# Two graph layers with residual layernorms: layernorm from VectorE's statistics instruction and one scale-and-shift per batch

## The chip, the cores and the metric

The kernel runs on one core of a Trainium2 chip. A core has TensorE (PE in the profile; PEld is its weight load), VectorE (DVE), ScalarE (ACT), GpSimd (POOL), SyncE (SP) and 16 DMA engines. Each engine works through its own instructions in a fixed order and waits for others by semaphores. The metric is device time in microseconds (us), the median of several runs.

## The reference

```python
def _layernorm(x, axis=-1, eps=1e-5):
    m = jnp.mean(x, axis=axis, keepdims=True)
    v = jnp.var(x, axis=axis, keepdims=True)
    return (x - m) / jnp.sqrt(v + eps)
...
# x: (8, 2048, 128), adj: (2048, 2048), mostly zero
# layer 0
res = si[:, :, None] + sj[:, None, :] + relation[None] * w_r + g_b
agg = jnp.einsum('bij,bjd->bid', res, inputs)
return agg @ weight + bias
...
# layer 1, with A1 = A2 = adj, orders = 2
x1 = jnp.einsum('bnf,nw->bwf', x0, A)
x2 = 2.0 * jnp.einsum('bnf,nw->bwf', x1, A) - x0
...
out = jax.nn.relu(x @ Theta1 + bias)
...
x = _layernorm(x + layer0(x, adj))
x = _layernorm(x + layer1(x, adj, adj))
```

Both layers end in a residual sum and a layernorm over the last axis, 128 numbers for each of 2048 nodes and 8 batches.

## The kernel before

Nodes are cut into 16 chunks of 128. A tile of a chunk holds 128 nodes on the partitions and 8 batches x 128 features, 1024 fp32 numbers, along the free axis. `HB` is 4: most steps go by halves of four batches (`h` is 0 or 1)[...].

The work goes in four stages.

1. **Load, 0 to about 165 us.** Rows of adj and chunks of x are loaded; PE transposes adj's blocks and multiplies x by the weights into `Y`. Masks of the nonzero tiles are made.
2. **Chunks 0 to 3, dense, to about 285 us** (L758). Each of four chunks takes all 16 blocks of adj. Beside this, DVE and PE build lists of the rows that hold nonzeros.
3. **Layer 0 over twelve listed chunks, about 285 to 480 us.** `seq` gives their order. For each: `own_rows` multiplies by the diagonal block (L819), and `listed_rows` multiplies gathered rows by small blocks (L837): for each half four matmuls of 32 columns, two of 64 and one of 128, so fourteen in all. Seven gathers by POOL (L629) bring these rows, from a DRAM copy of Y, into nine buffers that go round; three more gathers a chunk bring the blocks for a later chunk. Each matmul shows as two records in the trace.
4. **Layer 1, two hops** over all chunks (`hop`), to about 725 and to the end. Their listed rows are gathered from `u_d`, the first product of layer 0's output, and from `y_d`, the first hop's output. The second hop ends in a sum with a bias (L895), a relu with the residual (L896), a layernorm and the store of the output.

What lies around the layernorm in stage 3: `finish0` adds PSUM and the residual in two halves (L371), then calls `layernorm`. Its result `z` goes to `make_u` only in the next turn, as `pending`: eight transposes (`pt_p`, in the helper at L182), copied by DVE and ACT in turn (L174 and L176), eight products with Theta (`pp`, L388), copies by ACT (L391) and a store to `u_d` (L392). Nothing of the first hop's gathers can start before all of `u_d` is written.

`layernorm` (L202 to L218) is a chain over two engines: sum over features (L205, DVE), mean (L208), subtraction (L209), then for each half a square on ACT (L213) and its sum on DVE (L214), a square root on ACT (L215), a reciprocal (L217) and a product (L218). The squares share one buffer, so the second square waits for the first sum.

```python
        for h in range(2):
            hs = slice(h * HB, (h + 1) * HB)
            sq = small.tile([P, HB, D], F32, name=f"sq_{name}_{h}", tag="sq", bufs=1)
            nc.scalar.activation(sq, z[:, hs, :], AF.Square)
            nc.vector.tensor_reduce(st[:, 2, hs], sq, AX.X, ALU.add)
```

It runs 32 times: for chunks 0 to 3 in stage 2, for the twelve listed chunks, and for all sixteen in the second hop. In stage 2 the argument `pin` puts the first instruction behind a given one in DVE's order.

What sets the order: a scheduler lays out each engine's instructions ahead of time, from its own costs. Some orders are fixed by hand: the matmuls of `own_rows` and `listed_rows` among themselves (`in_order`), all gathers on POOL among themselves (`gather`), SP's loads (`keep_in_program_order`). Where the transposes and products of `make_u` stand among these matmuls is left to the scheduler. In the kernel before, a turn of stage 3 has on PE: the eight 32-column matmuls of chunk c+1, some of the transposes of chunk c, the 64- and 128-column matmuls of chunk c+1, the other transposes, and the products `pp`, with `own_rows` of the chunk after that around them.

A branch at the end (`many`) holds a dense version for other data. It isn't taken here.

Of the kernel before, what the change touches and what calls it, by code (L numbers as in the profile page):

```python
# [8 lines left out]
F32 = mybir.dt.float32  # L9
I32 = mybir.dt.int32  # L10
AF = mybir.ActivationFunctionType
ALU = mybir.AluOpType
AX = mybir.AxisListType
# [5 lines left out]
def kernel(  # L19
# [29 lines left out]
    nc = tc.nc  # L49
    P = 128  # L50
    B, N, D = x.shape
    NC = N // P
    NG = NC // 4
    HB = B // 2
# [29 lines left out]
    small = ctx.enter_context(tc.tile_pool(name="small", bufs=2))  # L84
# [19 lines left out]
    def rows4(name):  # L104
        return w4.tile([P, B, D], F32, name=name, tag="w4")
# [29 lines left out]
    epst = const.tile([P, 1], F32)  # L135
# [58 lines left out]
    def behind(ins, prev):  # L194

        tc.add_manual_dep(
            ins.ins, prev.ins.name,
            mybir.DependencyInfo(mybir.DependencyClass.NoSync, mybir.DependencyReason.DATA),
            reason="order",
        )  # L200

    def layernorm(z, name, pin=None):  # L202

        st = small.tile([P, 4, B], F32, name=f"st_{name}", tag="st")
        head = nc.vector.tensor_reduce(st[:, 0], z, AX.X, ALU.add)  # L205
        if pin is not None:
            behind(head, pin)
        nc.vector.tensor_scalar(st[:, 1], st[:, 0], 1.0 / D, None, op0=ALU.mult)  # L208
        nc.vector.tensor_sub(z, z, st[:, 1][:, :, None].to_broadcast([P, B, D]))  # L209
        for h in range(2):  # L210
            hs = slice(h * HB, (h + 1) * HB)
            sq = small.tile([P, HB, D], F32, name=f"sq_{name}_{h}", tag="sq", bufs=1)
            nc.scalar.activation(sq, z[:, hs, :], AF.Square)  # L213
            nc.vector.tensor_reduce(st[:, 2, hs], sq, AX.X, ALU.add)  # L214
        nc.scalar.activation(st[:, 3], st[:, 2], AF.Sqrt, bias=epst, scale=1.0 / D)  # L215
        rs = small.tile([P, B], F32, name=f"rs_{name}", tag="rs")
        nc.vector.reciprocal(rs, st[:, 3])  # L217
        nc.vector.tensor_mul(z, z, rs[:, :, None].to_broadcast([P, B, D]))  # L218

    def load_x(c, name, q, t=None):  # L220
        if t is None:
# [145 lines left out]
    def finish0(c, accs, xr, norm=True):  # L367

        for h in range(2):
            hs = slice(h * HB, (h + 1) * HB)  # L370
            nc.vector.tensor_add(xr[:, hs, :], accs[h], xr[:, hs, :])  # L371
        if norm:
            layernorm(xr, f"0_{c}")
        return xr
# [19 lines left out]
    def copy_r(n0, n1):  # L394
# [22 lines left out]
        op0=ALU.mult,  # L417
# [288 lines left out]
    for c in range(ND):  # L706
# [15 lines left out]
        else:  # L722
            z = finish0(c, accs, xr, c > 2)
        if c + 1 < ND:
            accs1, sit = acc_pair(), si_t(c + 1)
            at2 = first_at.get(c + 2)
            for j in range(NC):
                if c == 0:
                    if j == 4:
                        tile_ranks()  # L730
                    if j == 7:
                        tile_lists()
                    if j == 10:
                        at = tile_lists_end()
                        half_ranks()
                    if j == 14:
                        chunk_ranks()
                        z = finish0(c, accs, xr, False)
                        layernorm(z, "0_0", at)
# [5 lines left out]
                if c == 2:  # L745
                    if j == 4:
                        at = chunk_lists_end()
                        layernorm(z1, "0_1", at)
                    if j == 8:
                        layernorm(z, "0_2", at)  # L750
# [93 lines left out]
    with nc.allow_non_contiguous_dma(reason="512-byte rows of a diagonal block"):  # L844
        fetch_own(0, y0_d, seq[0])
        xr = load_x(seq[0], "xs", nc.sync)
        for c, c1 in zip(seq, seq[1:] + [None]):
# [10 lines left out]
            z = finish0(c, accs, xr)  # L858
# [83 lines left out]
    with tc.If(many == 1), nc.allow_non_contiguous_dma(reason="512-byte rows of a block"):  # L942
        for c in range(NC):
# [3 lines left out]
            z = finish0(c, accs, xr)  # L947
            nc.scalar.dma_start(out=x1_d[c * P:(c + 1) * P, :], in_=flat(z))
            make_u(c, z, rows4(f"xtd{c}"))
        for i, src in ((1, u_d), (2, y_d)):  # L950
            for c in range(NC):
# [9 lines left out]
                z = rows4(f"zd{i}_{c}")  # L961
                for h in range(2):
                    hs = slice(h * HB, (h + 1) * HB)
# [45 lines left out]
```

## Time and profile before

| what | value |
|---|---|
| median of 5 runs | 910.82 us (905.13 to 915.06) |
| the profiled execution | 913.96 us |
| its span in the trace | 912.2 us |
| PE busy | 779.5 us, 85% of the span |
| DVE busy | 405.3 us, 44% |
| ACT busy | 175.3 us, 19% |
| POOL busy | 439.1 us, 48% |
| data moved by DMA | 265.05 MB, mean 291 GB/s |
| mean granted TensorE clock | 0.943 |

A row of the groups, the waits or the timeline names the line, the engine, the operation, and what it writes and reads (`out<-in`), with partitions x elements. In the timeline a row starts with its start and length in us, and may end in brackets with how long the engine had been idle before and who let it go on. The layernorm's own rows, from the groups (busy us, then mean ns of one, then idle before it):

```profile
L214 DVE TENSOR_REDUCE st<-sq 128x4 f32<-128x512 f32 x64 | 43.9, 685 | 57.2 <-ACT sq L213 39.0
L213 ACT ACTIVATE sq<-z 128x512 f32<-128x512 f32 x32 | 20.1, 630 | 161.7 <-DVE z L209 112.5
```

The granted clock is the share of full speed that the throttle left to TensorE. Idle time of an engine that isn't the bottleneck costs nothing.

### The profile page before, as it was taken

The page shows a single profiled execution, that of the slowest core. Times are in us where ns is not written, and L with a number is a line of the kernel's source. Part 1 is how long each engine was busy: PE and PEld are TensorE (multiplying, and loading weights), DVE is VectorE, ACT ScalarE, POOL GpSimd, SP SyncE. Part 2 cuts the span into 40 slices and gives each one's busy share as a digit, 9 for nine tenths or more (in the row PEclk, how much of TensorE's full clock was granted, in tenths as well). Part 3 has the DMA queues.
Part 4 walks back from the last instruction along what each step waited for, and adds up shares of the span by engine and source line. Part 5 has one row for each costly group of instructions (what it writes and reads, how often), then busy time and mean ns, then how long its engine had stood idle before and what let it go on. Part 6 is the DMA issues. An engine that isn't in the chain of part 4 may idle for free. (4 is left out here: it accounts for less than half of the span.)

```text
span 912.2 us, 10299 instructions
## 1 busy us (share of the span) xinstructions
PE 779.5 (85%) x3607; PEld 382.6 (42%) x3607; DVE 405.3 (44%) x639; ACT 175.3 (19%) x397; POOL 439.1 (48%) x431
## 2 busy tenths in 40 slices
PE   5999989999996868687887888887999889999992
PEld 4666664465443333332344232332343334455430
DVE  5456673448962634455652000000100065776775
ACT  3666651011111212121211000000000010111111
POOL 0000000036577766477622766676664565676750
PEclk9999998999997978887999899999999999999996
DMA  8699999872658987899976788888998889999992
GB/s 285 213 307 317 332 297 302 264 267 78 216 200 310 342 305 264 296 317 312 342 315 198 263 282 303 293 314 298 352 383 313 296 295 326 363 346 357 349 333 78
DMA packets 171416, 265.05 MB, mean 291 GB/s; under 512 B 17069, under 2 KB 122069, under 8 KB 169180
## 3 DMA queue, kind: packets, MB, share of 16 engines
q0 software_dynamic: 49280, 148.61, 45.6%
q1 hardware_dynamic: 98746, 87.98, 30.0%
q10 hardware_dynamic: 23330, 27.73, 8.5%
q8 instruction: 30, 0.49, 0.2%
q14 instruction: 30, 0.25, 0.1%
HBM read 241.63 MB, written 60.96 MB: 332 GB/s over the span
## 5 line engine op out<-in xcount | busy, mean ns | idle before, releaser
L837 PE MATMUL acc<-Y,rc 128*32 128x512 f32 (+2 forms) x896 | 244.7, 626 | 43.0 <-issue 18.4
L629 POOL DMA_INDIRECT Y<-y_d,idx x196 | 210.8, 1075 | 120.7 <-PE acc L837 58.1
L629 POOL DMA_INDIRECT stage<-rr_d,idx x84 | 88.0, 1047 | 229.4 <-PE acc L758 206.5
L629 POOL DMA_INDIRECT Y<-u_d,idx x112 | 110.9, 990 | 88.3 <-DMA u_d<-rc 31.3
L837 PEld LDWEIGHTS acc<-Y,rc 128*32 128x32 f32 (+2 forms) x896 | 62.5, 130 | 214.4 <-issue 133.4
L837 PE MATMUL acc<-Y,rct 128*32 128x512 f32 (+2 forms) x336 | 89.6, 686 | 7.6 <-DMA Y<-y_d,idx 5.6
L758 PE MATMUL acc<-Y,wide 128*128 128x512 f32 x192 | 87.6, 606 | 0.0
L214 DVE TENSOR_REDUCE st<-sq 128x4 f32<-128x512 f32 x64 | 43.9, 685 | 57.2 <-ACT sq L213 39.0
L819 PE MATMUL acc<-Y,rd 128*128 128x512 f32 x140 | 67.9, 597 | 0.0
L174 DVE COPY z<-acc 128x512 f32<-128x512 f32 x9 | 6.2, 692 | 136.9 <-remote 65.7
L758 PEld LDWEIGHTS acc<-Y,wide 128*128 128x128 f32 x192 | 36.0, 195 | 39.8 <-issue 39.8
L213 ACT ACTIVATE sq<-z 128x512 f32<-128x512 f32 x32 | 20.1, 630 | 161.7 <-DVE z L209 112.5
L837 PEld LDWEIGHTS acc<-Y,rct 128*32 128x32 f32 (+2 forms) x336 | 22.8, 144 | 60.5 <-issue 45.0
L182 PE MATMUL pt_a<-ident,rc 128*128 128x128 f32 x240 | 35.9, 286 | 6.6 <-DMA rc<-in_adj_dram 6.2
L319 PE MATMUL acc<-wx,tr_x 128*128 128x130 f32 x256 | 36.8, 287 | 4.2 <-ACT tr_x L176 3.4
L290 DVE TENSOR_REDUCE rc<-rc 128x64 f32<-128x2048 f32 x16 | 36.5, 2279 | 6.3 <-DMA rc<-in_adj_dram 6.3
L182 PE MATMUL pt_p<-ident,xs 128*128 128x128 f32 x96 | 16.0, 289 | 27.1 <-DVE xs L218 24.2
L319 PEld LDWEIGHTS acc<-wx,tr_x 128*128 128x128 f32 x256 | 32.9, 195 | 14.5 <-ACT tr_x L176 6.7
L329 PE MATMUL acc<-Y,wide 128*128 128x512 f32 x64 | 36.1, 646 | 2.5 <-ACT Y L323 1.4
L371 DVE TENSOR_TENSOR xs<-acc,xs 128x512 f32<-128x512 f32 x24 | 16.6, 692 | 48.1 <-PE acc L837 26.0
L298 DVE TENSOR_REDUCE stage<-rct 128x64 f32<-128x2048 f32 x12 | 27.4, 2286 | 20.5 <-ACT rct L176 20.5
L182 PEld LDWEIGHTS pt_a<-ident,rc 128*128 128x128 f32 x240 | 29.5, 148 | 16.0 <-issue 14.7
(204 smaller groups left out, 908.0 us busy)
## 6 DMA issues: line engine op xcount, KB each, us to landing
rc<-in_adj_dram SPq DMA_DIRECT2D x16, 1024.0 KB
rr_d<-rct SPq DMA_DIRECT2D x12, 1024.0 KB
rr_d<-in_adj_dram SPq DMA_DIRECT2D x12, 1024.0 KB
xs<-in_x_dram SPq DMA_DIRECT2D x20, 512.0 KB
y_d<-Y SPq DMA_DIRECT2D x16, 512.0 KB
out_dram<-z ACTq DMA_DIRECT2D x16, 512.0 KB
u_d<-u ACTq DMA_DIRECT2D x14, 512.0 KB
Y<-y_d SPq DMA_DIRECT2D x14, 512.0 KB
```

The lines of the kernel that those rows point to most:

```text
L182: nc.tensor.transpose(pt[:, i, :], s, ident)
L213: nc.scalar.activation(sq, z[:, hs, :], AF.Square)
L214: nc.vector.tensor_reduce(st[:, 2, hs], sq, AX.X, ALU.add)
L290: nc.vector.tensor_reduce(mk[:, c, :], a.rearrange("p (w f) -> p w f", f=TW), AX.X, ALU.max, apply_absolute_value=True,)
L298: nc.vector.tensor_reduce(mkt[:, :, 4 * c:4 * c + 4], at.rearrange("p j (t f) -> p j t f", f=TW), AX.X, ALU.max, apply_absolute_value=True,)
L319: nc.tensor.matmul(py[:, i, 0:D + 2], xt[b // HB][:, (b + i) % HB, :], wx, start=True, stop=True,)
L329: nc.tensor.matmul(acc0[h], first_at[0][:, c, :], Y[c][:, h * HB:(h + 1) * HB, :], start=(c == 0), stop=False, skip_group_check=True,)
L371: nc.vector.tensor_add(xr[:, hs, :], accs[h], xr[:, hs, :])
L629: g = nc.gpsimd.indirect_dma_start(out=out, out_offset=None, in_=src, in_offset=bass.IndirectOffsetOnAxis(ap=ids[:, n:n + 1], axis=0), bou ...
L758: mm = nc.tensor.matmul(accs1[h], at1[:, j, :], Y[j][:, h * HB:(h + 1) * HB, :], start=(j == 0), stop=False, skip_group_check=True,)
L819: in_order(nc.tensor.matmul(accs[h], r, t[:, h * HB:(h + 1) * HB, :], start=start, stop=False, skip_group_check=True,))
L837: in_order(nc.tensor.matmul(accs[h][w * t:w * t + w], r[:, o + w * t:o + w * t + w], gs[t][:, h * HB * D:(h + 1) * HB * D], start=False, s ...
```

## The change

Only `layernorm` is edited. The sums and squares go; VectorE's statistics instruction (`bn_stats`) is called once per batch on 128 numbers and writes six: a count, a mean and a sum of squared deviations for the numbers in even places, and the same for those in odd places. A few instructions on 8 numbers per partition join the two halves: the sum of squared deviations of all 128 is the sum of the two plus 32 times the squared gap between the means. From this come r = 1 / sqrt(variance + eps) and -m r. One instruction per batch then gives z r - m r in place, for batches 1, 4 and 6 on ACT and for the other five on DVE. The buffer of squares is no longer needed.

```diff
-        st = small.tile([P, 4, B], F32, name=f"st_{name}", tag="st")
-        head = nc.vector.tensor_reduce(st[:, 0], z, AX.X, ALU.add)
-        if pin is not None:
-            behind(head, pin)
-        nc.vector.tensor_scalar(st[:, 1], st[:, 0], 1.0 / D, None, op0=ALU.mult)
-        nc.vector.tensor_sub(z, z, st[:, 1][:, :, None].to_broadcast([P, B, D]))
-        for h in range(2):
-            hs = slice(h * HB, (h + 1) * HB)
-            sq = small.tile([P, HB, D], F32, name=f"sq_{name}_{h}", tag="sq", bufs=1)
-            nc.scalar.activation(sq, z[:, hs, :], AF.Square)
-            nc.vector.tensor_reduce(st[:, 2, hs], sq, AX.X, ALU.add)
-        nc.scalar.activation(st[:, 3], st[:, 2], AF.Sqrt, bias=epst, scale=1.0 / D)
-        rs = small.tile([P, B], F32, name=f"rs_{name}", tag="rs")
-        nc.vector.reciprocal(rs, st[:, 3])
-        nc.vector.tensor_mul(z, z, rs[:, :, None].to_broadcast([P, B, D]))
+        nb = z.shape[1]
+        st = small.tile([P, B, 6], F32, name=f"st_{name}", tag="st")[:, 0:nb]
+        for b in range(nb):
+            head = nc.vector.bn_stats(st[:, b], z[:, b])
+            if pin is not None:
+                behind(head, pin)
+        m0, m1, v0, v1, gap, var = [st[:, :, n] for n in (1, 4, 2, 5, 0, 3)]
+        nc.vector.tensor_sub(gap, m0, m1)
+        nc.vector.tensor_add(var, v0, v1)
+        nc.vector.scalar_tensor_tensor(gap, gap, D / 4.0, gap, op0=ALU.mult, op1=ALU.mult)
+        nc.vector.tensor_add(var, var, gap)
+        nc.scalar.activation(v0, var, AF.Sqrt, bias=epst, scale=1.0 / D)
+        nc.vector.tensor_add(m0, m0, m1)
+        nc.vector.reciprocal(v1, v0)
+        nc.vector.scalar_tensor_tensor(m1, m0, -0.5, v1, op0=ALU.mult, op1=ALU.mult)
+        for b in range(nb):
+            if b % 8 in (1, 4, 6):
+                nc.scalar.activation(
+                    z[:, b], z[:, b], AF.Identity, bias=m1[:, b:b + 1], scale=v1[:, b:b + 1]
+                )
+            else:
+                nc.vector.tensor_scalar(
+                    z[:, b], z[:, b], v1[:, b:b + 1], m1[:, b:b + 1], op0=ALU.mult, op1=ALU.add
+                )
```

No other line changes. The scheduler, whose costs see other instructions, lays out the engines anew: in a turn of stage 3, PE now has two of the 32-column matmuls of chunk c+1, the eight transposes of chunk c with one 32-column matmul among them, the other five, the products `pp` among the 64-column matmuls, and the 128-column ones last. POOL's and SP's orders are the same as before.

## The prediction

> **What bounds the kernel now.** I read the page's slices first, to see which stages have slack, then the stage table, PE's waits in the stage that has it, the timeline of one turn there, and the end of the timeline.
>
> ```profile
> PE   5999989999996868687887888887999889999992
> ...
> PEclk9999998999997978887999899999999999999996
> DMA  8699999872658987899976788888998889999992
> ```
>
> Each digit is 1/40 of the span. PE is full until slice 13 and again from slice 32 on. The hole in between has two parts: 285 to 480 us (layer 0 over the listed chunks, with a layernorm in each turn) and the first Chebyshev hop up to 725 us, which has no layernorm. So the change can act in the first part, and in the last digit, the end.
>
> ```profile
> 290.00:480.00 190.00, 145.84 (x680) 66.85 (x679) 94.95 (x160) 37.23 (x69) 115.13 (x106) 0.88 0.87 312
> 335.00:350.00 15.00, 10.15 (x45) 5.43 (x46) 7.00 (x12) 3.12 (x6) 5.98 (x5) 0.69 0.59 207
> 455.00:470.00 15.00, 10.48 (x60) 4.85 (x56) 9.61 (x17) 3.75 (x8) 5.97 (x5) 1.00 1.03 404
> ```
>
> These are rows of the stage table (window, length, busy PE, PEld, DVE, ACT, POOL, granted clock, DMA share, GB/s). PE is idle for 44 of 190 us, but the transfers are busy 0.87 of the time: twelve 15 us windows from 290 to 470 average 0.90, from 0.59 to 1.03. There is slack, and not much.
>
> ```profile
> PE pt_p L182 <- DVE xs L218: 24.2, 9, 4.5
> PE pp L388 <- DVE wide L174: 5.4, 1, 5.4
> PE pp L388 <- ACT wide L176: 4.1, 2, 2.1
> PE pp L388 <- issue: 4.0, 1, 4.0
> ```
>
> PE's waits from 290 to 500 us: 24.2 us for the layernorm's last instruction (L218), and 13.5 us before the products pp, whose input copies stand in DVE's and ACT's queues behind the sums of L371 or the squares. One turn shows the loop:
>
> ```profile
> 444.68 0.41 PE L182 MATMUL pt_p<-ident,xs 128*128 128x128 f32 x2 [2.99 <-DVE xs L218]
> 445.02 3.85 PE L837 MATMUL acc<-Y,rct 128*64 128x512 f32 x12
> 448.05 0.69 DVE L371 TENSOR_TENSOR xs<-acc,xs 128x512 f32<-128x512 f32 x1 [2.63 <-PE acc L837]
> 450.11 1.21 DVE L205 TENSOR_REDUCE st<-xs 128x8 f32<-128x1024 f32 x1
> 456.55 1.22 DVE L218 TENSOR_TENSOR xs<-xs,rs 128x1024 f32<-128x1024 f32 x1
> 457.93 0.41 PE L182 MATMUL pt_p<-ident,xs 128*128 128x128 f32 x2 [2.85 <-DVE xs L218]
> ```
>
> PE's order is fixed: the rest of the next chunk's matmuls stands behind the transposes of the last chunk's normalized rows. So a turn is sum, layernorm, transposes, 3.85 us of matmuls, sum: 13.25 us here. L205's first start is 300.0 and its twelfth 477.7, so the mean turn is 177.7/11 = 16.2 us.
>
> ```profile
> 493.77 0.98 POOL L629 DMA_INDIRECT Y<-u_d,idx  x1 [31.25 <-DMA u_d<-rc]
> ```
>
> The next hop's first gather waits until the last layernorm's product is stored: the end of that stage is a pure chain through it. So is the end of the kernel:
>
> ```profile
> 893.28 1.04 PE L894 MATMUL pt_r<-ident,Y 128*128 128x128 f32 x8
> ...
> 899.39 1.22 DVE L205 TENSOR_REDUCE st<-z 128x8 f32<-128x1024 f32 x1
> ...
> 902.17 0.63 ACT L213 ACTIVATE sq<-z 128x512 f32<-128x512 f32 x1 [6.70 <-DVE z L209]
> ...
> 904.21 0.69 DVE L214 TENSOR_REDUCE st<-sq 128x4 f32<-128x512 f32 x1 [0.70 <-ACT sq L213]
> ...
> 905.50 1.22 DVE L218 TENSOR_TENSOR z<-z,rs 128x1024 f32<-128x1024 f32 x1
> 906.76 0.38 ACTq L903 DMA_DIRECT2D out_dram<-z  x1
> ```
>
> PE ends at 894.3, but DVE still has a layernorm in hand and starts the last at 899.39. It takes 7.33 us to 906.72.
>
> **What the Trainium skill says.** "VectorE: DVE Perf Modes", The TRN2 errata: an fp32 tensor_tensor takes (N+151)/0.96 ns. The trace agrees: 692 for 512 columns, 1226 for 1024. The same page, The DRAIN you can't avoid: the next operation waits for the pipe, unless it is not held. Here independent 128x128 operations of 0.28 us start 0.20 apart (444.45, 444.65), dependent ones 0.02 to 0.03 after the other's end. "ScalarE: Activation LUTs", What ACT_TABLE_LOAD costs: 186 ns + 0.833 N, 93 more for each pointer operand, and back-to-back ones overlap by 93. The trace's L215 (N 8, one pointer) took 301, near the 286 of that. The same page, Table sets: identity is in every set, so no reload is due; the trace has one load before L215, of 1.283 us, and none later between square and square root. No page prices the statistics instruction.
>
> **The change, part by part.** Each of the 32 layernorms loses L205, L208, L209, two squares with their reductions, L217 and L218 (7.33 us as a chain, DVE 5.4 and ACT 1.56 us busy). It gains:
> - Eight statistics of 128 columns. No row shows one. At one column a cycle like L205 I take 0.20 apart and 0.29 each; below that 0.13 apart if it ran at two columns, above 0.33 if it goes over its data twice, 0.5 if worse. The first falls between the two sums; seven remain: 7 x 0.20 + 0.09 = 1.5 us.
> - Small 128x8 steps at L208's 0.17, two pairs overlapping: 0.6 us. Square root 0.30 and two handovers: 0.36. Reciprocal 0.20 and the product 0.17, with gaps: 0.42.
> - Apply: DVE 4 x 0.20 + 0.28 = 1.1 us; ACT three with two pointers, an estimate by the ScalarE page of 479 ns spaced 386: 1.25, with handover 1.3. They run side by side.
>
> Sum 4.2 us for 7.33, and busy DVE 4.9, ACT 1.74. ACT's extra 0.2 us lies in its idle time. I take no double rate for the pointer-scalar steps: L663, the same form, took 280 to 343 ns, no less than a tensor_tensor's 287.
>
> **End.** The last sums need PE's 894.3, so L896 ends at 895.0. DVE is free by then: the previous layernorm ends near 892 (884.9 + 2.6 of sums + 4.2). 895.0 + 8 x 0.20 + 0.09 + 2.7 = 899.4 for 906.7: **-7.3 us**. The last store behind it is unchanged.
>
> **Stage end.** From the last L371's end, 477.2, 4.2 us lead to 481.4; the transposes started at 485.94, behind PE work that ends near 480 in the new order. The stored product and the gather follow: **-4 us**.
>
> **Turns of the listed stage.** The scheduler also moves PE work: the transposes now stand behind only two of the eight 32-column matmuls, and six of these (1.92 x 6/8 = 1.4 us) and all of pp (1.8 us) come behind the transposes, ahead of the wider matmuls. POOL's and SP's orders are unchanged. So part of the gain is handed back. Old turn at full clock 13.25. New: transposes 0.9 + 1.4 + 1.8 + 3.4 of wider matmuls up to the first sum, then 0.9 to the second, 0.7 for it and 4.2: 13.3 by plain addition; transposes, products and matmuls overlap at their joints as these records do, so I take 12.6, 0.65 less, or 7 us over 11 turns. Still about 2.8 us of PE waiting per turn: the layernorm is shorter, but has less in front of it. What should go besides is part of the 13.5 us before pp, since pp's copies now have 1.4 us of matmuls as cover, and the squares no longer stand in ACT's queue. If that cover is gone, up to 13.5 us come back. The ceiling is the transfers: 180 us at 0.90 need 166 at 0.97, so at most 14 us. POOL is near too: ten gathers a turn, 1.05 + 0.30 each, make 13.5 us. Both are late next. I take **-8 us**, bounds -14 and +4.
>
> **Second hop.** From 725 to 880 us PE is busy for 151.2 of 155 and the transfers 0.96, DVE 102: the shorter layernorm is hidden. If that cover went, DVE's 6.8 us a chunk would still be under PE's 10. Zero; likewise before 285 us, where PE is busy for 117 of 125 (at best -2).
>
> Sum: -19.3 us against the profiled execution, 913.96 us (span 912.2): 894.7. That run was 0.3% above the median, 910.82, so the forecast is 910.82 x 894.7/913.96 = **891.5 us**.
>
> **Rivals**, in median time.
> - The stage gains nothing, since the transfers and POOL hold its turn: only the two chains, -11.3: 899.5. For it: windows at 0.97 to 1.03. Against: one at 0.59.
> - The stage reaches the transfers' ceiling and a cheaper statistic helps both chains: -14, -5, -8.5: 883.4.
> - A statistic goes over its data twice, 0.33 apart: turns lengthen by 0.9, past the 0.65 won, +3 us; the end gains 6.3, the stage end 3: about 904.5, no change.
> - **Slower**: the statistic costs 0.5 or more. The place is pt_p at L182. Each layernorm grows by 2.1 us, and PE, with the 3.2 us that used to precede or run beside it now behind the transposes, holds back the next chunk's sums and the gather buffers. It decides from 0.29 apart (0.65/7 above 0.20). At 0.5: turn +1.45 x 12 = +17; end -4.9, stage end -2: about +10, 921. If PE is at half clock in those 3.2 us too, +3 a turn, a dearer 0.33 would do.
> - That the change doesn't do what it says: no, both the instructions and their moved order are in the program.
>
> **How the numbers follow.** Changes within 1% can't be told from none (five runs spread from 905.1 to 915.1). Chances: forecast 0.57, no stage gain 0.18, ceiling 0.09, two passes 0.10, slower 0.06. Faster takes the first, the ceiling and half of the second: 0.76; slower 0.06; within 1% 0.18. The range, 877 to 905, takes in the ceiling with 6 us more of front and stage, and the two-pass case.
>
> **What would show it.** Statistics of 0.29 us starting 0.20 apart; last layernorm 4.2 us, from 895; PE's waits at pt_p still near 2.8 us a turn, those before pp gone; turns of about 15.5 us; the first gather of u_d some 12 us earlier; the second hop as long as before. Wrong if the statistic is over 0.3 apart, or if pt_p waits over 4 us a turn with POOL idle behind it.

## The result, and the profile after

The changed kernel takes **903.02 us** (median of 41 runs, 896.0 to 909.3). The kernel before takes 908.63 in the runs beside them (78 runs, 899.8 to 925.0). The medians differ by 5.6 us. The ratio is 0.9951, 95% interval 0.9935 to 0.9966, which is 4.5 us; it leaves out executions over 1.5% above the fastest of their kernel. Forecast were 19.3 us less, 891.5.

The profiled execution of the changed kernel took 901.61 us, 1.4 below its median; that of the kernel before took 913.96, 5.3 above its own. So the two traces differ by 12.3 us, more than the medians. First the slices of the changed kernel's page, to set beside those of before:

```profile
PE   5999989999992898989897878888988899999994
...
PEclk9999998999996899999999898989999999999998
DMA  8699999982567999999985788888999689999994
```

PE is fuller in slices 15, 17, 19 and 21, and one digit fell to 2: slice 13, at 270 to 292 us. The granted clock is higher in slices 15 to 20, where the kernel before has digits of 7 and 8. The stage table's row from 290 to 480 us (length, busy PE, PEld, DVE, ACT, POOL, clock, DMA share, GB/s) and PE's waits from 290 to 500 us:

```profile
290.00:480.00 190.00, 171.07 (x717) 72.90 (x718) 83.80 (x333) 41.63 (x87) 103.88 (x105) 0.98 0.91 319
```

```profile
PE pp L397 <- issue: 16.4, 1, 16.4
PE pt_p L182 <- issue: 10.6, 7, 2.5
PE acc L846 <- DMA Y<-u_d,idx: 6.1, 2, 3.4
PE pt_p L182 <- PE acc L846: 5.4, 4, 1.4
```

PE's 24.2 us before the transposes pt_p shrank to 16.0, and the small waits at pp are gone. But PE is busy for 171 us where it was for 146, which is 17% more, with 5% more matmul records in the window (717 for 680): the first sign that its matmuls cost more. And one wait of 16.4 us at pp is new. It ends at 292.8 and explains the digit 2 of slice 13.

The layernorm itself is as short as forecast. A row of the groups (busy, mean ns), then the end of the timeline and the first gather of the first hop:

```profile
L207 DVE BATCH_NORM_STATS2 st<-z 128x6 f32<-128x128 f32 x128 | 26.2, 278 | 0.0
```

```profile
486.51 0.99 POOL L638 DMA_INDIRECT Y<-u_d,idx  x1 [27.17 <-DMA u_d<-rc]
...
889.88 1.64 DVE L207 BATCH_NORM_STATS2 st<-z 128x6 f32<-128x128 f32 x8
...
892.98 1.37 DVE L225 TENSOR_SCALAR z<-z,st 128x128 f32<-128x128 f32 x5
...
894.43 0.38 ACTq L912 DMA_DIRECT2D out_dram<-z  x1
```

Eight statistics take 1.64 us, so they start 0.20 apart; the last layernorm goes from 889.88 to 894.35, 4.5 us (forecast 4.2).

The same kernels ran later on other chips. These come in two kinds: on the **slower** ones the kernel before takes 908 to 913 us, as in the result above, on the **quicker** ones 878 to 880. Cut at the same points, the traces give (us; the quicker chip's are the runs b_again and a_again below):

| stretch | slower: before, after | change | quicker: before, after | change |
|---|---|---|---|---|
| start to the first second-half sum of stage 3 | 299.3, 305.7 | +6.4 | 301.3, 300.6 | -0.7 |
| eleven turns | 177.2, 168.9 | -8.3 | 156.7, 164.7 | +7.9 |
| last sum to first gather of u_d | 17.2, 11.9 | -5.4 | 17.3, 11.9 | -5.4 |
| first hop | 217.3, 218.8 | +1.5 | 204.9, 204.9 | 0 |
| second hop to the last transposes | 182.2, 182.6 | +0.4 | 179.2, 182.7 | +3.5 |
| last transposes to last store | 13.5, 6.5 | -6.9 | 10.4, 6.5 | -3.8 |

The places where the gain goes are the turns, the front (the first row) and, on the quicker chip, the second hop.

### The profile page after: what moved, and what is told of

Read it like the earlier page. It is cut to its first block, busy times and chain, and to the rows that moved or that the text cites. A ratio compares the mean times of both kernels' runs of the same rounds, so it can differ in the third digit from the quotient of the medians.

```text
span 899.8 us, 10724 instructions
## 1 busy us (share of the span) xinstructions
PE 795.0 (88%) x3607; PEld 382.4 (42%) x3607; DVE 360.9 (40%) x1055; ACT 176.9 (20%) x429; POOL 420.4 (47%) x431
## 5 line engine op out<-in xcount | busy, mean ns | idle before, releaser
L638 POOL DMA_INDIRECT Y<-y_d,idx x196 | 194.7, 994 | 135.9 <-PE acc L846 74.5
L638 POOL DMA_INDIRECT stage<-rr_d,idx x84 | 84.9, 1011 | 229.5 <-DMA y_d<-Y 187.5
L846 PE MATMUL acc<-Y,rct 128*32 128x512 f32 (+2 forms) x336 | 105.5, 622 | 0.0
L828 PE MATMUL acc<-Y,rd 128*128 128x512 f32 x140 | 66.0, 593 | 0.0
L215 ACT ACTIVATE st<-st,epst 128x8 f32<-128x8 f32 x32 | 9.9, 309 | 234.6 <-DVE st L214 71.8
L380 DVE TENSOR_TENSOR xs<-acc,xs 128x512 f32<-128x512 f32 x24 | 16.4, 683 | 82.0 <-issue 36.0
L905 DVE SCALAR_TENSOR_TENSOR z<-z,pt_r 128x512 f32<-128x512 f32 x32 | 20.6, 683 | 51.7 <-PE pt_r L903 18.7
L328 PEld LDWEIGHTS acc<-wx,tr_x 128*128 128x128 f32 x256 | 32.9, 195 | 14.4 <-ACT tr_x L176 6.4
L885 PEld LDWEIGHTS acc<-th,wide 128*128 128x128 f32 x256 | 31.5, 192 | 8.1 <-issue 8.1
```

The lines of the kernel that those rows point to most:

```text
L328: nc.tensor.matmul(py[:, i, 0:D + 2], xt[b // HB][:, (b + i) % HB, :], wx, start=True, stop=True,)
L638: g = nc.gpsimd.indirect_dma_start(out=out, out_offset=None, in_=src, in_offset=bass.IndirectOffsetOnAxis(ap=ids[:, n:n + 1], axis=0), bou ...
L828: in_order(nc.tensor.matmul(accs[h], r, t[:, h * HB:(h + 1) * HB, :], start=start, stop=False, skip_group_check=True,))
L846: in_order(nc.tensor.matmul(accs[h][w * t:w * t + w], r[:, o + w * t:o + w * t + w], gs[t][:, h * HB * D:(h + 1) * HB * D], start=False, s ...
L885: in_order(nc.tensor.matmul(accs[h][:, b, :], x1t[c][:, h * HB + b, :], th[:, i, :], start=(b == 0), stop=False, skip_group_check=True,))
L905: nc.vector.scalar_tensor_tensor(z[:, hs, :], z[:, hs, :], 0.0, pt, op0=ALU.max, op1=ALU.add)
```

## What a turn of the changed kernel shows

One turn, 414.27 to 429.47 us, from the timelines of DVE and PE, and ahead of it a row of the kernel before. `x10` counts records, two to a matmul:

```profile
439.77 1.92 PE L837 MATMUL acc<-Y,rct 128*32 128x512 f32 x16
```

```profile
414.27 0.69 DVE L380 TENSOR_TENSOR xs<-acc,xs 128x512 f32<-128x512 f32 x1 [6.97 <-issue]
...
416.73 1.05 PE L846 MATMUL acc<-Y,rct 128*32 128x512 f32 x4
419.14 0.90 PE L182 MATMUL pt_p<-ident,xs 128*128 128x128 f32 x5 [1.35 <-PE acc L846]
419.98 1.04 PE L846 MATMUL acc<-Y,rct 128*32 128x512 f32 x2
420.95 0.55 PE L182 MATMUL pt_p<-ident,xs 128*128 128x128 f32 x3
421.43 1.90 PE L846 MATMUL acc<-Y,rct 128*32 128x512 f32 x10
423.26 0.94 PE L397 MATMUL pp<-th,wide 128*128 128x128 f32 x6
424.13 1.07 PE L846 MATMUL acc<-Y,rct 128*64 128x512 f32 x2
425.13 0.94 PE L397 MATMUL pp<-th,wide 128*128 128x128 f32 x6
426.00 1.93 PE L846 MATMUL acc<-Y,rct 128*64 128x512 f32 x6
427.86 0.71 PE L397 MATMUL pp<-th,wide 128*128 128x128 f32 x4
428.40 1.88 PE L846 MATMUL acc<-Y,rct 128*128 128x512 f32 x4
...
429.47 0.69 DVE L380 TENSOR_TENSOR xs<-acc,xs 128x512 f32<-128x512 f32 x1 [6.98 <-PE pp L397]
```

A single 32-column matmul (x2) takes 1.04 us, and five (x10) take 1.90. In the kernel before, all eight together (x16) took 1.92. They are meant to run four at a time, in four strips of columns: a **group** takes as long as one of its members. Here the transposes cut the eight into pieces of 2, 1 and 5: 1.05 + 1.04 + 1.90 = 4.0 us. The products cut the 64-column pairs likewise: 1.07 + 1.93 = 3.0 us for four, which need 1.9. The Trainium skill, "TensorE: Matmul & The Clock Gate", Packing small matmuls, says that matmuls in different strips overlap, and that PE never reorders matmuls. These rows agree with both.

So a turn is 4.87 us from the first sum to the transposes and 10.33 of PE without a gap from there to the next sum: 15.20. The eight turns from 338 to 460 us are 15.19 to 15.20 each, and so are eight in the changed kernel's trace on a quicker chip. The turns of the kernel before do not repeat like that: in its trace the eleven are 13.2 to 20.1 us long.

The granted clock is a second thing in which the old turns differ. The eleven turns of the kernel before and of the changed one (columns as in the stage table), and a row of wider matmuls of the kernel before, twelve records like those that took 3.85 us in the turn of the prediction:

```profile
299.30:476.50 177.20, 133.04 (x605) 59.04 (x604) 90.16 (x153) 34.89 (x65) 109.18 (x100) 0.87 0.88 315
```

```profile
305.70:474.60 168.90, 152.85 (x630) 62.82 (x630) 74.11 (x298) 37.23 (x78) 96.35 (x97) 0.99 0.91 323
```

```profile
397.43 6.17 PE L837 MATMUL acc<-Y,rct 128*64 128x512 f32 x12
```

From 395.4 to 402.2 us the granted clock was 0.50. In the trace of the kernel before, the three turns in which it never fell took 13.2, 13.4 and 14.0 us, the other eight 14.4 to 20.1. An estimate from the rows' means: a clock of 0.87 over 177 us costs up to 23 us of full-speed time, one of 0.99 over 169 us up to 2. On another slower chip the old turns had 0.91 (175.5 us, the run b2_again below). What makes the clock fall is not shown here.

## Experiments

Ratios are to the kernel before on the same chip, run beside each trial, with 95% intervals; a gain in us is taken from the ratio, unless two medians are named. First the parts alone, on a quicker chip. A line in `layernorm` sends some of its invocations to the old text, placed at the end of the file (its `st` has six rows in place of four, the rest is unchanged):

```diff
     def layernorm(z, name, pin=None):
+        if name[0] != "1": return layernorm_old(nc, small, behind, epst, z, name, pin)
```

That is the end alone; the others differ in the condition on the name.

**New in the second hop alone.**

> The new layernorm for the sixteen chunks of the second hop alone, the old one for all others. PE's order is then that of the kernel before. The prediction's end term says -7.3 us against the kernel before, all of it between the last PE work and the last store (in the traces that stretch fell from 13.5 to 6.6 us). Rival, the second hop is not free of the layernorm after all: then the change in time differs from -7 by over 2 us, and the stretch from the first gather of y_d to the last transposes (182.2 us before) moves.

Measured 0.9976 (0.9955 to 0.9996): -2.1 us, not -7.3. Two things account for the rest. On this chip the old end is short too: 10.8 and 11.0 us in the next two runs, 6.5 here. And the rival holds: the hop to the last transposes takes 181.4 us, against 177.9 and 179.6 in these two, which have the old layernorm there.

**New in the listed chunks alone.**

> The new layernorm for the twelve listed chunks of layer 0 alone. PE's order in the turns is then that of the changed kernel, the front's that of the kernel before. The prediction's two terms: turns -8, stage end -4, so -12 us. First rival, the time of the changed kernel is lost in the front: here -12 too, with the first sums (L380) near 298.6 us as in the kernel before, not 304.8. Second rival, the two traces are single executions and the turns gain little in the median: 0 to -3 us, with turns still at 15.4 us in some executions and over 16 in others.

Measured 1.0027 (1.0012 to 1.0042): slower by 2.4 us. Neither theory had that. The turns take 164.7 us, at 15.20 each, against 157.6 in the run before this one, whose turns are the old ones.

**New in the four dense chunks alone.**

> The new layernorm for the four dense chunks alone; beyond the first turn PE's order is that of the kernel before. Prediction: 0 (at best -2). First rival, the order of the front: the square root of chunk 3 now stands between the two copies of u1 on ACT, and the copy of chunk 2's transposes behind that layernorm on DVE, so +6 us, with PE standing some 16 us before pp and the first sums near 304.8 us instead of 298.6. Second rival, the late front of the changed kernel's trace is a matter of that one execution: 0, first sums near 298.6.

Measured 0.9942 (0.9922 to 0.9962): 5.1 us less; first sums at 298.4. On this chip the front isn't late. What the 5.1 us are isn't settled: this trace and the others of its kind differ by 2 us in the front and less elsewhere.

**New everywhere but there.**

> The new layernorm everywhere but for the four dense chunks. If the front's order costs 6 us, this is 6 us shorter than the changed kernel (903.0): near 897, -12 us against the kernel before; by the prediction's whole sum even -19, near 890. If the front costs nothing in the median, the same as the changed kernel, -5.6 us.

Measured 0.9998 (0.9984 to 1.0013). This is e1 and e2 added: -2.1 + 2.4.

**Both kernels again, on a quicker chip.**

> The kernel before, for a trace beside the others of this call; timed against itself it must give a ratio of 1. It gives the anchors (first sums, eleven turns, first gather of u_d, hops, end) on the chip on which the edits are run. If the end in it, from the last transposes to the last store, is 11 us instead of 13.5, the end term of the prediction was read from one execution.

> The changed kernel again, beside the others. If the turns are locked by PE's order, they are 15.20 us here as in the first trace, whatever the chip; if transfers set them, they are 14.3 or less, as those of the kernel with the new layernorm in the second hop alone. From the parts run alone (end -2.1, listed chunks +2.4, first four -5.1) the sum is -4.8 us against the kernel before; if parts don't add up, 0 or -10.

The kernel before against itself: 0.9994 (0.9975 to 1.0012). The changed kernel: 0.9995 (0.9978 to 1.0012), so **no gain at all** on this chip. The parts' sum, about -5 us, is not found again: they ran on one quicker chip and this on another, and which of the two, the chip or the sum, is at fault stays open. The end is indeed 10.4 us here and not 13.5; the turns are 15.19. From 300 to 455 us (columns as above), the kernel before and the changed one:

```profile
300.00:455.00 155.00, 131.62 (x608) 57.01 (x608) 90.09 (x153) 35.23 (x66) 109.85 (x100) 0.97 0.97 357
```

```profile
300.00:455.00 155.00, 141.82 (x586) 58.06 (x584) 70.54 (x288) 34.90 (x74) 96.56 (x97) 1.00 0.96 342
```

PE is busier by 10 us while fewer of its records (586 against 608) fall into the window.

**Whole groups.** PE's order in the listed turns, written by hand, with the new layernorm:

```diff
-            nc.tensor.transpose(pt[:, i, :], s, ident)
+            hold[0](nc.tensor.transpose(pt[:, i, :], s, ident))
...
     def make_u(c, z, xt, u=None, part=0):
+        hold[0] = in_order if part else (lambda mm: mm)
...
             gs = [rows_of(a + n * c + t) for t in range(n)]
+            n == 2 and mid and mid()
...
-            listed_rows(0, y0_d, c, accs)
-            make_u(*pending)
+            listed_rows(0, y0_d, c, accs, len(pending) == 4 and (lambda: make_u(*pending, 1)))
+            make_u(*pending, *[2][:len(pending) == 4])
```

Part 1 of `make_u` is the transposes, part 2 the products and the store. The lines on `hold` and the parts that are left out do the same for the products. The first listed turn keeps the scheduler's order.

> The changed kernel with PE's order in the turns written by hand: the eight 32-column matmuls together, then the eight transposes, the four 64- and two 128-column matmuls together, then the products. In the changed kernel's trace six 32-column matmuls behind the first transpose took 2.94 us, where all eight take 1.92 together, and a 64-column pair split by a product took 1.07 more. Theory, the split groups cost the turns about 3 us of PE on the path: turns of 13.0 to 13.5 us (ten gathers of 1.30 on POOL are then the bound), PE busy about 10.7 us a turn instead of 13.9, -20 us against the changed kernel. Rival, the transfers bind as soon as PE does not: turns of 14.3, -10 us. Second rival, the split does not matter and the layernorm's chain sets 15.2: no change.

Measured **0.9867** (0.9845 to 0.9889), -11.3 us between the medians, 866.8 and 878.1. The eleven turns take 153.1 us, 13.9 each: less than the rival's 14.3, and more than the 12.3 us a turn for which PE is busy. The transfers leave little room: over the eleven turns the DMA share is 0.99, against 0.96 over the old turns on this chip.

**The same order with the old layernorm.**

> The old layernorm everywhere, with the same order by hand for PE. If the order is worth the gain and not the layernorm, this is as fast as the new layernorm with that order, but for the end. By the chain, sums 1.6, layernorm 7.3, transposes 1.4 and 2.9 of wider matmuls make turns of 13.2 us: within 2 us of the kernel before, which had 13 to 14.3 on a chip like this. If the old layernorm's length counts in the turns, they are over 14.

Measured 0.9997 (0.9977 to 1.0018); turns 159.5 us, 14.5 each. So on this chip the order alone gives nothing and the layernorm alone gives nothing (0.9995), while both together give 1.3%: the short layernorm is worth something here only if PE's groups stay whole.

**Whole groups, but transposes and products early.** To tell the split from the new place of the transposes, this order keeps them ahead of the wider matmuls: four 32-column matmuls, the eight transposes, the other four, the products, then the rest.

```diff
             for h in range(2):
+                (n, h) == (4, 1) and mid and mid(1)
+                (n, h) == (2, 0) and mid and mid(2)
```

> The changed kernel with PE's order by hand, but close to its own: the transposes stand between the two halves of the 32-column matmuls and the products ahead of the 64-column ones, as in the changed kernel, only that no group of 32- or 64-column matmuls is split. If the split groups cost the time, the turn is 15.2 less some 3 us of PE on the path, so what the transfers allow: near 13.9 as in the other unsplit order, -10 us against the changed kernel. If the place of the transposes and products ahead of the wider matmuls costs it, turns stay near 15 and the time within 3 us of the changed kernel (0.9995 of the kernel before).

Measured **0.9803** (0.9762 to 0.9844), on a slower chip: 891.95 us for 910.16, where the changed kernel had 0.9951. Part of a turn:

```profile
402.88 1.31 PE L182 MATMUL pt_p<-ident,xs 128*128 128x128 f32 x8 [0.68 <-issue]
404.11 1.07 PE L847 MATMUL acc<-Y,rct 128*32 128x512 f32 x8
405.25 2.05 PE L397 MATMUL pp<-th,wide 128*128 128x128 f32 x16
407.23 3.85 PE L847 MATMUL acc<-Y,rct 128*64 128x512 f32 x12
```

Four 32-column matmuls (x8) take 1.07, as long as one took alone. The eleven turns take 161.2 us against 168.9, with transposes and products near the places that the changed kernel gives them, and with DVE's and ACT's order in a turn as in the changed kernel. Nor is it the granted clock, which is 0.97 from 300 to 470 us here and was 0.99 over the turns of the changed kernel. It is the split that costs, not the place.

The same kernel ran twice more on another slower chip, as a base for the next trials:

> The kernel with whole groups and PE's order close to the changed kernel's, once more, as the base of the next two: 0.980 to 0.987 of the kernel before. First sums at 305 to 308 where the kernel before takes 910 us, near 299 where it takes 879.

> The kernel with whole groups as the base of the next two. Where the kernel before takes 879 us: 0.987 of it, second-hop turns of 11.0 us. Where it takes 910: 0.980 to 0.987.

Measured 0.9872 (0.983 to 0.9914) and 0.9866 (0.9811 to 0.9921), turns 164.4 and 161.3 us.

**The front.** In nine traces of kernels with the new layernorm of chunk 3 on slower chips, the first sums come at 304.0 to 310.7 us; in the two of the kernel before, at 298.6 and 301.0. On quicker chips all lie from 298.4 to 301.4. The trial gives the four dense chunks their old layernorm back, with whole groups:

> The kernel before once more, for its trace beside the others of this call: ratio 1. If its first sums (L371) come at 305 us too, the late front is the chip's and not the layernorm's; at 298 to 301, it is the changed kernel's.

> The same with the old layernorm for the four dense chunks. If chunk 3's new layernorm delays the front: where the kernel before takes 910 us, first sums near 298.6 and 6 us less than the run with whole groups; where it takes 879, the same time. If the front is a matter of the execution: first sums as in that run, and the same time within 2 us.

The kernel before against itself gave 1.0007 (0.9982 to 1.0033). The trial gave **0.9781** (0.9743 to 0.982), 893.6 us; the base beside it 901.2. So on this chip the old layernorm in the dense chunks was worth 7.6 us between the medians of six runs each, and 4.3 us between the two traces. The same base reached 0.9803 on another slower chip (e7) with the new layernorm there, so the size is uncertain. The timeline of the kernel before, then of the base:

```profile
277.80 0.59 ACT L391 COPY u<-pp 128x512 f32<-128x512 f32 x1 [3.15 <-PE pt_p L182]
279.99 0.59 ACT L391 COPY u<-pp 128x512 f32<-128x512 f32 x1 [1.60 <-remote]
...
281.44 0.69 DVE L174 COPY xt<-pt_p 128x512 f32<-128x512 f32 x1 [4.43 <-remote]
```

```profile
284.37 0.59 ACT L400 COPY u<-pp 128x512 f32<-128x512 f32 x1 [11.10 <-remote]
284.85 0.31 ACT L215 ACTIVATE st<-st,epst 128x8 f32<-128x8 f32 x1
294.94 0.59 ACT L400 COPY u<-pp 128x512 f32<-128x512 f32 x1 [9.78 <-remote]
...
296.41 0.69 DVE L174 COPY xt<-pt_p 128x512 f32<-128x512 f32 x1 [10.80 <-remote]
...
297.25 2.05 PE L397 MATMUL pp<-th,xt 128*128 128x128 f32 x8 [20.23 <-DVE xt L174]
```

In the new order chunk 3's square root (L215) stands between the two copies of u1 on ACT. On DVE, its reciprocal waits for that root and stands ahead of the copy of chunk 2's transposes, on which PE waits 20 us. In the old order that copy stands ahead of the layernorm's second half, at 281.4. In the trial it ran at 281.25 again, and the first sums came at 304.7 instead of 309.3. But the order is not the wait that ends last: in the base DVE was done with the reciprocal and the product behind it at 285.6 and stood idle for another 10.80 us before the copy, and in the changed kernel's first trace for 12.12. The matmuls that these copies read ended by 278 in PE's records of all three. The trace's semaphore records, which no view prints, show that the copies wait for a count that PE itself raises: in the base at 284.34, 294.92 and 296.38 us, in the kernel before at 277.78, 279.97 and 281.42. On the quicker chip of e5 the same copies ran at 274.1, 275.0 and 275.4, within 0.1 us of the ends in PE's records.

The granted clock goes with it. In every trace it falls to 0.50 between 278 and 284 us. It stays there for 10.2 us in both traces of the kernel before and for 6.8 to 10.2 on quicker chips, but for 13.7 to 20.5 in the nine with late first sums, and in the trial for 10.2 and once more for 6.8 us, from 297.0. There, six records of 64-column matmuls took 3.68 us, for 1.93 in the turn above. Whether the lower clock holds PE back here or only goes with its long wait is not shown. Why PE's counts come late on the slower chips stays **open**, and with it how much of the late front is the layernorm's: the trial's first sums, with the old one, are still 3.7 us behind those of the kernel before (301.0).

**The second hop.** In four traces on quicker chips with the old layernorm there (b_again, e2, e3, e6) the turns between 720 and 850 us take 10.5 to 10.7 us, in four with the new one (a_again, e1, e4, e5) 10.9 to 11.0. PE's order is fixed by hand there. Kernel before, then changed, one chunk each (PE's transposes, the store's issue, PE's listed matmuls):

```profile
769.38 1.04 PE L894 MATMUL pt_r<-ident,wide 128*128 128x128 f32 x8
770.34 5.75 PE L837 MATMUL acc<-Y,rc 128*32 128x512 f32 x28
...
769.23 0.38 ACTq L903 DMA_DIRECT2D out_dram<-z  x1
```

```profile
770.76 1.04 PE L903 MATMUL pt_r<-ident,wide 128*128 128x128 f32 x8
771.73 6.81 PE L846 MATMUL acc<-Y,rc 128*32 128x512 f32 x28
...
766.79 0.38 ACTq L912 DMA_DIRECT2D out_dram<-z  x1
```

The listed matmuls of a chunk take longer with the new layernorm, and the store of the chunk before leaves 4 us ahead of the transposes instead of with them. Whether this store collides with the gathers was to be shown by giving the hop its old layernorm but for the last chunk, and by holding the stores:

```diff
+                for store in late:
+                    tc.add_manual_dep(
+                        store().ins, mms[-1].ins.name,
+                        mybir.DependencyInfo(
+                            mybir.DependencyClass.Sync, mybir.DependencyReason.DATA
+                        ), reason="pace",
+                    )
```

> The kernel with whole groups (0.987 of the kernel before) with the old layernorm in the second hop, except for its last chunk. In eight traces of one kind of chip the hop's middle has turns of 10.5 us with the old layernorm and 11.0 with the new, though PE's order is the same, and the end is 4 us shorter. If the new layernorm lengthens the hop, here the hop has 10.5 again (-5 us) and the short end stays: 0.981, some 862 where the kernel before has 878. If the turns differ for other reasons: 0.987 or above.

> The kernel with whole groups and the new layernorm everywhere, but each store of the second hop waits until PE has ended the matmuls ahead of the next chunk's transposes. With the old layernorm it left 0.2 us ahead of these transposes; with the new it leaves 4 us earlier, in the middle of a chunk's gathers. If that collision lengthens the hop: turns of 10.5 us, -5 us, 0.981. If not (DVE's or ACT's own work in the hop does it): 0.987, turns of 11.0.

> The same with new layernorms everywhere and the second hop's stores held until the matmuls ahead of the next chunk's transposes are done. If the earlier stores lengthen the hop: turns of 10.5 us instead of 11.0 and 4 to 5 us less than the run with whole groups, where the kernel before takes 879 us. If they don't: the same time within 2 us.

> The same with the old layernorm in the second hop except for its last chunk. Where the kernel before takes 879 us: turns of 10.5 us and 4 us less than the base if the new layernorm lengthens the hop, the same if not. Where it takes 910: the same within 3 us, as the turns did not differ there.

> The base with the second hop's stores held until the matmuls ahead of the next chunk's transposes are done. Where the kernel before takes 879 us: 4 us less than the base and turns of 10.5 us if the stores are what lengthens the hop; the same as the base with turns of 11.0 if it is the layernorm's own work. Where it takes 910: the same.

All five fell on slower chips. Old layernorm in the hop: 0.989 (0.9848 to 0.9932) in e8 and 0.9903 (0.9874 to 0.9932) in e14, beside e13's 0.9866. Held stores: 0.9811 (0.9768 to 0.9853) in e9; 0.9861 (0.9819 to 0.9903) in e12 beside e10's 0.9872; 0.9859 (0.9795 to 0.9923) in e15 beside e13: the same. (e8 and e9 have e5's order, so they are set beside each other; e12, e14 and e15 have that of e7.) On slower chips the hop gains nothing from either, and the old layernorm there looks slower, by 2.4 us between the medians of e14 and e13 and by 5.6 between those of e8 and e9. Its turns from 757 to 868 us are 10.6 to 10.8 us in e7, e10, e13 and b2_again alike. On the quicker chips, where the hop does lengthen, neither was run: the cause there stays open.

The best version of the slower chips is thus the new layernorm in the listed chunks and the second hop, the old one in the dense chunks, and whole groups: 0.9781, an interval that overlaps e7's. It wasn't run on a quicker chip.

## Why the prediction was right or wrong

The direction was right and 903.0 lies in the range; the gain was under a third of the forecast, and on a quicker chip it is none. Between the two traces of the slower chips it is 12.3 us of the 19.3. The 7.0 that are missing there are the front, 6.4, and the two hops, 1.9, less 1.3 by which the two ends and the turns came out better together.

- **Statistics, small steps, apply: right.** 276 ns at 0.20 apart; small steps 0.17; the apply 1.37 us on DVE (forecast 1.1; one takes 0.34, and they start 0.26 apart) beside 1.26 on ACT. An estimate for ACT's instruction, from the Trainium skill's "ScalarE: Activation LUTs", What ACT_TABLE_LOAD costs, was 479 ns; measured 483. The rivals on a dear statistic are ruled out.
- **Stage end, -4: right in kind, -5.4 on both chips.**
- **End, -7.3: -6.9 on the slower chip, -3.8 on the quicker.** The term had two parts: a layernorm of 4.2 instead of 7.33, and DVE no longer busy with the chunk before. The second is there only where the old layernorms pile up at the end; on the quicker chip they don't.
- **Turns, -8: the number came on the slower chip, by luck.** The step that failed is the price "six of these (1.92 x 6/8 = 1.4 us)". Six matmuls of groups cut by transposes took 2.94, the four 64-column ones, cut by products, 3.0 and not 1.9: 2.6 us of the difference between 10.33 us from transposes to first sum and the 7.5 that the prediction added up. The change of order was seen, but its price was scaled by the count of matmuls, not of groups. The turns then lock at 15.20, where the forecast for a full-clock turn was 12.6: a loss of 2 us on the old full-clock turn, 13.25, and not a gain of 0.65. On the quicker chip it comes as one, 15.0 on the mean for 14.25. On the slower chip the old mean was 16.1, with a granted clock of 0.87, and the changed kernel's turns run at 0.99. The sum left the old excess over 13.25 in place; that it went is not in it. With whole groups the mean is 14.7 (e7) and 13.9 (e5).
- **"Zero; likewise before 285 us": this step failed too, +6.4 on the slower chip.** Busy PE was taken as cover, with the averages of a window that ends where PE runs dry: from 276 us it had nothing but the products behind one copy. The trial with the old layernorm, 4.3 to 7.6 us better on one chip, says that the new one has a part in it; how large the part is, and why PE's own counts come late there, stays open.
- **Second hop, zero: +0.4 on the slower chip, right; +3.5 on the quicker**, cause open.
- **From one execution to the median.** The forecast scaled the whole sum from an execution that proved to be 5.3 us above the median of 78 runs, not 3. The difference between two traces, -12.3, is thus not what the change is worth: 5.3 and 1.4 of it are the distances of these executions from their medians.
- **Slips without weight.** The last division gives 891.6, not 891.5, and the shares of "faster" and "within 1%" add up to 0.75 and 0.19. L663's 280 to 343 ns are means of two groups; single ones took 273 to 380. DVE's busy time per layernorm fell from 5.4 to 4.0 us, not to 4.9: instructions that overlap were added up.

With the two losses taken away on the slower chips the ratio is 0.980 to 0.987 (whole groups) and 0.978 (with the front's old layernorm as well), 18.9 us between the medians. That this is near the forecast is not the forecast come true: it takes an order of PE that the forecast did not have, and the front is still late.

What was to show it: the statistics, the last layernorm (4.5 us) and the turns (15.36 on the mean) came near what was written. The waits at pt_p did not: they should have stayed near 2.8 us a turn and are 1.35 in the locked turns, since from the first sum to the transposes it is 4.87 us there and not the 5.8 of the sum (0.9 + 0.7 + 4.2). The first gather of u_d came 7.3 us earlier and not 12, since the front had lost 6.4, and at pp one wait of 16.4 us was new. The list lacked the one number that would have told at once, PE's busy time per turn: 12.1 us before, 13.9 after.

## What to carry to other kernels

Where a scheduler lays out PE, shortening a step on another engine can move transposes into a group of column-packed matmuls; price a moved matmul by the groups that it cuts, not by its share of a sum, and pin the groups. A window in which an engine is busy on average covers nothing at its edge: read what the engine waits for next there, and what that waits for. Compare the granted clock of a stage before and after, ahead of crediting its change to a sum of durations. And run both kernels on more than one chip before a gain of half a per cent is believed.

## What the runs showed of the hardware

- One 32-column matmul of 512 columns alone took 1.04 us, four neighbours in different column strips 1.07, eight 1.92. Other matmuls between them cut the group: in pieces of 2, 1 and 5 the eight took 4.0.
- Twelve records of wider matmuls took 3.85 us in one turn of the kernel before and 6.17 in another, in which the granted clock fell to 0.50.
- The statistics instruction on 128 fp32 numbers takes 276 ns, 0.20 from one to the next. For 1024 numbers that is 1.64 us, where a plain sum of them took 1.22.
- The same program takes 878 to 880 us on two chips and 908 to 913 on others, and a change that gave 0.5% on one of these gave nothing on one of the quicker two.
